# A graph and expert-mixture kernel on one core: in the second graph stage, each panel's products are issued ahead of the rest of the panel before, and the preparation is divided between two engines

## The chip, the cores and the metric

The kernel runs on one core of a Trainium2 chip. The metric is device time in microseconds. Three runs before the change gave 1915.95, 1919.1 and 1920.69 us; the median is 1919.1 us. The engines are PE (matrix products), DVE (vector), ACT (scalar and table functions), POOL (GpSimd) and SP (which here only starts transfers).

## The reference

The input is `x` with 3125 nodes of 256 features, and 50000 edges `src -> dst`. Four blocks follow each other, each of them normalizing `x`, computing something, and adding it to `x`:

```python
x = x + L0_gnn(layernorm(x))     # two mean-aggregating graph convolutions, one product
x = x + L0_ffn(layernorm(x))     # 16 experts, two chosen for each node
x = x + L1_gnn(layernorm(x))     # the second graph stage: the change is here
x = x + L1_ffn(layernorm(x))     # 8 experts, two chosen for each node

# L1_gnn, with P = 64 and K = 3
x_static = x[:, :P]
for i in range(K):               # degree-normalized convolution with self-loops
    x_static = relu(gcn_conv(x_static, src, dst, W_static[i], b_static[i]))
ew = gelu(x @ W1 + b1) @ W2 + b2
x_dyn = segment_sum(x[:, :P][dst] * ew[src], src)
out = concatenate([x_static + x_dyn, x[:, P:]]) @ W_aggr + b_aggr
```

## The kernel before

The nodes are padded to 3200, that is 25 tiles of 128, and grouped in seven panels: six of 512 columns and one of 128. Earlier in the kernel the edges have been counted into a dense matrix of small integers, kept on the chip as 8-bit numbers (`at8`, one tile for each panel). A graph convolution is then a product of the node features with this matrix.

The second graph stage has these parts.

*Preparation* (L1042 to L1052). For each panel the rows are loaded from `xb0` (SP, L1045) and normalized: statistics on DVE (L387, L388), a square root on ACT (L390), a reciprocal (L391) and one subtract-and-multiply for each tile on DVE (L393). POOL's `split` (L428, L429) writes the first 64 features as a rounded number and its remainder into `xc`. Each tile is transposed on PE (L401) and copied by ACT (L402) into `xT`, one tile for all panels. DVE scales the 64 features by `dinv` (L1051), and `split` writes them into `g0`. The rows have two buffers and the scaled features one.

*Branch.* `second_graph` is built twice, for exact and for rounded operands. A flag chooses at run time; the traced execution takes the rounded form. Within the branch ACT first issues the loads of the weights and biases.

*Passes* (three, the loop over `i`). For each panel, PE multiplies 25 blocks of the matrix with the features (`pc`, L1136). Each block of 8-bit numbers is first cast to 32 bits: of five blocks ACT casts two (L434), DVE two (L436) and POOL one (L438); there are five block buffers. The product with the identity (L1142) adds the self-loops. ACT copies `pc` to `gT` (L1147). In passes 1 and 2, four small products with the weights follow (`pw`, L1151), then three steps on DVE (L1156, L1157, L1161: scale, bias, rectify and scale) and POOL's `split` into the features of the next pass. In pass 3 the product is made the other way round, with features along partitions (`pwT`, L1167): `dinv` is spread by four products with the identity (`pi`, L1172), ACT copies it, DVE multiplies, ACT adds the bias and rectifies (L1179), DVE adds the result to `xT` (L1180), and `finish` follows.

*dynamic* runs for four panels after pass 1 and for three after pass 2. It computes `ew` and the dynamic part, for which the matrix is transposed on PE (L474), and writes it over the first 64 features in `xT`.

*finish* makes a panel's output: the rows are loaded again (L1112), `product` with `W_aggr` (`po`, L413), two additions on DVE (L1116 for the bias, L1117), a store, a normalization (into `rows`, one buffer), a store, a transposition of each tile and the gate scores (`pg`, L413; L489), and then the router's `panel` (L526 to L589), a chain of small DVE steps with two small products in it (`ranks`, L568 and L569).

The order on each engine is not that of the source. A scheduler places the instructions of a branch in one fixed order for each engine at build time; at run time each engine takes its own instructions strictly in that order. In pass 3 this order puts `pwT` of a panel directly behind the first `ranks` product of the panel before it.

Of the kernel before, what the change touches and what calls it, by code (L numbers as in the profile page):

```python
# [8 lines left out]
F32 = mybir.dt.float32  # L9
# [9 lines left out]
P = 128  # L19
# [33 lines left out]
def kernel(ctx: ExitStack, tc: tile.TileContext, a, out: bass.AP):  # L53
# [325 lines left out]
            nc.vector.tensor_copy(deg, pdeg)  # L379


    def normalize(dst, x, n):

        mv = work.tile([P, TPP, 2], F32, name="mv")
        st = work.tile([P, TPP, 6], F32, name="st")
        for i in range(n):
            nc.vector.bn_stats(st[:, i, :], x[:, i, :])  # L387
            nc.vector.bn_aggr(mv[:, i, :], st[:, i, :])  # L388
        rstd = work.tile([P, TPP], F32, name="rstd")
        nc.scalar.activation(rstd[:, :n], mv[:, :n, 1], AF.Sqrt, bias=eps)  # L390
        nc.vector.reciprocal(rstd[:, :n], rstd[:, :n])  # L391
        for i in range(n):
            nc.vector.tensor_scalar(  # L393
                dst[:, i, :], x[:, i, :], mv[:, i, 0:1], rstd[:, i : i + 1], op0=OP.subtract, op1=OP.mult
            )

# [10 lines left out]
    def rows_in(ap, c0, w):  # L407
        return ap[c0 : c0 + w, :].rearrange("(t p) d -> p t d", p=P)
# [626 lines left out]

    with ExitStack() as c:
        gp = c.enter_context(tc.tile_pool(name="gp", bufs=1))
        xp = c.enter_context(tc.tile_pool(name="xp1", bufs=2))
        open_rows(c, 1)
        xT = gp.tile([P, KD, NP], F32, name="xT")  # L1040
        g0, g1, xc = (gp.tile([P, NT, 2, CD], F32, name=n) for n in ("g0", "g1", "xc"))
        for c0, w in PANELS:  # L1042
            n, t0 = w // P, c0 // P
            rows = xp.tile([P, TPP, D], F32, name="x")
            nc.sync.dma_start(rows[:, :n, :], rows_in(xb0, c0, w))  # L1045
            normalize(rows, rows, n)
            split(xc[:, t0 : t0 + n, 0, :], xc[:, t0 : t0 + n, 1, :], rows[:, :n, :CD])
            g = xp.tile([P, TPP, CD], F32, name="g", bufs=1)
            for i in range(n):
                transpose_tile(xT[:, :, c0 + i * P : c0 + (i + 1) * P], rows[:, i, :])  # L1050
                nc.vector.tensor_scalar(g[:, i, :], rows[:, i, :CD], dinv[:, t0 + i : t0 + i + 1], None, op0=OP.mult)  # L1051
            split(g0[:, t0 : t0 + n, 0, :], g0[:, t0 : t0 + n, 1, :], g[:, :n, :])  # L1052

        def second_graph(exact):
            one = F32 if exact else F32R
            with ExitStack() as c:
                loads = c.enter_context(tc.tile_pool(name="loads1", bufs=3))
                cw = c.enter_context(tc.tile_pool(name="cw1", bufs=1))
                small = c.enter_context(tc.tile_pool(name="small1", bufs=1))
# [5 lines left out]
                        ws[i * CD : (i + 1) * CD], a["L1_gnn_W_static"].rearrange("i p q -> p i q")  # L1065
                    )
                bs = row_of(cw, "L1_gnn_b_static", 3 * CD)
                bs2 = cw.tile([CD, 1], F32, name="bs2")
                nc.scalar.dma_start(bs2, a["L1_gnn_b_static"][2:3, :].rearrange("i (p o) -> p (i o)", o=1))
                wd1 = weight(cw, "L1_gnn_W1", P)  # L1070
                bd1 = cw.tile([P, 1], F32, name="bd1")
                nc.scalar.dma_start(bd1, a["L1_gnn_b1"].rearrange("(p o) -> p o", o=1))
# [9 lines left out]
                def dynamic(c0, w):  # L1082
# [2 lines left out]
                    pe = ps_one("pe1", [P, PW])  # L1085
                    for k in range(KD):
                        nc.tensor.matmul(  # L1087
                            pe[:, :w], wd1[:, k, :], xT[:, k, c0 : c0 + w], start=(k == 0), stop=(k == KD - 1)
                        )
                    e1 = gw.tile([P, PW], F32, tag="wide", name="e1")  # L1090
                    nc.scalar.activation(e1[:, :w], pe[:, :w], AF.Gelu, bias=bd1)
# [11 lines left out]
                    nc.scalar.copy(both[:, :w], pd[:, :w])  # L1103
                    pf = ps_one("pf", [CD, PW])
                    nc.tensor.matmul(pf[:, :w], fold, both[:, :w], start=True, stop=True)
                    nc.vector.tensor_mul(xT[:CD, 0, c0 : c0 + w], ew[:, :w], pf[:, :w])

                def finish(c0, w):

                    n, t0 = w // P, c0 // P  # L1110
                    x = xp.tile([P, TPP, D], F32, name="x")
                    nc.sync.dma_start(x[:, :n, :], rows_in(xb0, c0, w))  # L1112
                    for i in range(n):
                        po = ps_one("po", [P, D])
                        product(po, xT[:, :, c0 + i * P : c0 + (i + 1) * P], wa)
                        nc.vector.tensor_add(x[:, i, :], x[:, i, :], ba)  # L1116
                        nc.vector.tensor_add(x[:, i, :], x[:, i, :], po)  # L1117
                    nc.sync.dma_start(rows_in(xb1, c0, w), x[:, :n, :])
                    rows = rows_tile()
                    normalize(rows, x, n)  # L1120
                    nc.sync.dma_start(rows_in(xnd1, c0, w), rows[:, :n, :])
                    s = small.tile([P, TPP, NE1], F32, name="s")[:, :n, :]
                    for i in range(n):
                        nT = gw.tile([P, KD, P], F32, name="nT", bufs=1)
                        transpose_tile(nT, rows[:, i, :])
                        scores(s[:, i, :], nT, gw1, gb1, NE1)
                    router1.panel(small, c0, s)

                g = g0
                for i in range(3):  # L1130
                    nxt = g1 if i == 0 else g0
                    for c0, w in PANELS:
                        n, t0 = w // P, c0 // P
                        pc = ps_wide("pc")[:, 0, :]
                        for k, blk in panel_of(exact, loads, c0, w, True):
                            nc.tensor.matmul(  # L1136
                                pc[:, :w], g[:, k].rearrange("p i q -> p (i q)").bitcast(one), blk,
                                start=(k == 0), stop=False,
                            )
                        for t in tiles_of(c0, w):  # L1140
                            o = t * P - c0
                            nc.tensor.matmul(  # L1142
                                pc[:, o : o + P], g[:, t].rearrange("p i q -> p (i q)").bitcast(one), identr.bitcast(one),
                                start=False, stop=(o + P == w),
                            )
                        gT = gw.tile([P, PW], F32, tag="wide", name="gT")
                        nc.scalar.copy(gT[:, :w], pc[:, :w])  # L1147
                        if i < 2:
                            pw = ps_one("pw", [P, TPP, CD])
                            for o in range(n):  # L1150
                                nc.tensor.matmul(  # L1151
                                    pw[:, o, :], gT[:, o * P : (o + 1) * P], ws[:, i, :], start=True, stop=True
                                )
                            s = dinv[:, t0 : t0 + n, None].to_broadcast([P, n, CD])
                            v = gw.tile([P, TPP, CD], F32, name="v")
                            nc.vector.tensor_tensor(v[:, :n, :], pw[:, :n, :], s, OP.mult)  # L1156
                            nc.vector.tensor_tensor(  # L1157
                                v[:, :n, :], v[:, :n, :],
                                bs[:, None, i * CD : (i + 1) * CD].to_broadcast([P, n, CD]), OP.add,
                            )  # L1160
                            nc.vector.scalar_tensor_tensor(  # L1161
                                v[:, :n, :], v[:, :n, :], 0.0, s, op0=OP.max, op1=OP.mult
                            )
                            split(nxt[:, t0 : t0 + n, 0, :], nxt[:, t0 : t0 + n, 1, :], v[:, :n, :])
                        else:
                            pw = ps_one("pwT", [CD, PW])
                            nc.tensor.matmul(pw[:, :w], ws[:, i, :], gT[:, :w], start=True, stop=True)  # L1167

                            pi = ps_one("pi", [CD, PW])
                            for t in tiles_of(c0, w):  # L1170
                                o = t * P - c0
                                nc.tensor.matmul(  # L1172
                                    pi[:, o : o + P], dinv[:, t : t + 1].to_broadcast([P, CD]), ident,
                                    start=True, stop=True,
                                )
                            v = gw.tile([CD, PW], F32, tag="wide", name="vT")
                            nc.scalar.copy(v[:, :w], pi[:, :w])
                            nc.vector.tensor_mul(v[:, :w], v[:, :w], pw[:, :w])
                            nc.scalar.activation(v[:, :w], v[:, :w], AF.Relu, bias=bs2)  # L1179
                            nc.vector.tensor_add(xT[:CD, 0, c0 : c0 + w], xT[:CD, 0, c0 : c0 + w], v[:, :w])  # L1180
                            finish(c0, w)
                    if i < 2:
                        g = nxt
                        for c0, w in PANELS[4 * i : 4 * i + 4]:
# [62 lines left out]
```

## Time and profile before

| | us |
|---|---|
| median of three runs | 1919.1 |
| the profiled execution | 1919.9 |
| its span, first to last instruction | 1918.1 |
| mean granted TensorE clock | 0.92 |
| busy: PE / DVE / ACT / POOL | 1652.2 / 893.1 / 682.5 / 509.8 |
| preparation: first load to last copy | 1079.3 to 1117.5 |
| passes 1, 2, 3: first product | 1130.4, 1279.3, 1394.9 |
| last `po` | 1565.8 |

Times inside a trace are counted from the span's start. A line of the timeline gives start, duration, engine, source line, operation, output and input tile, the count of merged instructions, and in brackets the idle time of the engine before it with the instruction that ended the wait. "x8" on PE means eight passes: a 32-bit product takes two of them.

### The profile page before, as it was taken

The numbers are of one execution on the slowest core, as the hardware profiler recorded it, in microseconds if no ns is written. First come the engines' busy times: TensorE is split into PE (matmuls) and PEld (weight loads), VectorE is DVE, ScalarE is ACT, GpSimd is POOL, SyncE is SP. The second block draws the span as 40 slices with busy tenths as digits, with TensorE's granted clock in tenths as the row PEclk, the third lists the DMA queues.
The fourth block names the chain that finished last, engine by engine and source line by source line (L and its number), as shares of the span: only waits on it lengthen the run. The fifth ranks groups of instructions, "written<-read, shape, count | busy, mean of one in ns | idle before, by whom it ended". The sixth has DMA issues, their size and how long they took to land. (4 is left out here: it accounts for less than half of the span.)

```text
span 1918.1 us, 24044 instructions
## 1 busy us (share of the span) xinstructions
PE 1652.2 (86%) x7618; PEld 1127.4 (59%) x7618; DVE 893.1 (47%) x2509; ACT 682.5 (36%) x1596; POOL 509.8 (27%) x543
## 2 busy tenths in 40 slices
PE   4899999799998399999999459789797647999995
PEld 3777777677777155665556336456565534556553
DVE  5866665246665423322233457456467452222221
ACT  2766666234442122222222246346363102222221
POOL 4411110100000334444443234014021202445442
PEclk9999999999998599999999769999998657999998
DMA  3311111611110687777777220000012603444444
GB/s 116 104 47 47 48 48 37 224 59 56 56 59 24 202 247 216 218 213 211 211 217 192 63 60 0 1 1 1 1 34 66 233 28 76 102 102 99 101 103 102
DMA packets 126765, 193.02 MB, mean 101 GB/s; under 512 B 15040, under 2 KB 71727, under 8 KB 126559
## 3 DMA queue, kind: packets, MB, share of 16 engines
q1 hardware_dynamic: 93036, 137.34, 22.6%
q0 software_dynamic: 28544, 50.74, 12.7%
q10 hardware_dynamic: 5042, 3.23, 0.6%
q8 instruction: 67, 1.10, 0.2%
q14 instruction: 76, 0.61, 0.1%
HBM read 148.74 MB, written 45.72 MB: 101 GB/s over the span
## 5 line engine op out<-in xcount | busy, mean ns | idle before, releaser
L723 PE MATMUL pa<-blk,hl 128*128 128x512 f32 (+1 forms) x1400 | 366.9, 401 | 1.3 <-ACT blk L434 1.3
L997 POOL DMA_INDIRECT xb<-y,idx x120 | 190.9, 1591 | 326.7 <-DVE each L992 221.2
L723 PEld LDWEIGHTS pa<-blk,hl 128*128 128x128 f32 x1400 | 249.3, 196 | 43.7 <-ACT blk L434 1.8
L434 ACT CAST blk<-at 128x512 fp32r<-128x512 fp8e4 (+1 forms) x378 | 208.3, 572 | 137.2 <-PE pa L723 59.4
L961 PE MATMUL ph<-w,xT 128*128 128x512 f32 x512 | 238.8, 610 | 5.6 <-ACT xT L402 0.8
L980 PE MATMUL pe<-w_all,hTs 128*128 x960 | 227.2, 379 | 3.0 <-ACT hTs L976 3.0
L980 PEld LDWEIGHTS pe<-w_all,hTs 128*128 128x128 f32 x960 | 182.1, 190 | 78.1 <-issue 55.5
L436 DVE CAST blk<-at 128x512 fp32r<-128x512 fp8e4 (+1 forms) x392 | 167.8, 438 | 93.2 <-PE pa L723 56.4
L1136 PE MATMUL pc<-blk,g 128*128 128x512 f32 (+1 forms) x525 | 150.2, 420 | 23.9 <-ACT blk L434 13.7
L940 POOL DMA_INDIRECT xg<-xnd,idx x120 | 117.9, 982 | 168.4 <-DVE idx L661 86.0
L961 PEld LDWEIGHTS ph<-w,xT 128*128 128x128 f32 x512 | 92.6, 191 | 114.4 <-issue 88.3
L402 ACT COPY xT<-pt 128x256 f32<-128x256 f32 x195 | 72.6, 372 | 227.8 <-PE pt L401 226.0
L1027 DVE TENSOR_TENSOR hid<-hid,ph 128x512 f32<-128x512 f32 x64 | 44.0, 688 | 232.8 <-ACT hid L1026 232.8
L438 POOL CAST blk<-at 128x512 fp32r<-128x512 fp8e4 (+1 forms) x105 | 66.1, 629 | 292.2 <-PE pc L1136 290.3
L1136 PEld LDWEIGHTS pc<-blk,g 128*128 128x128 f32 x525 | 92.7, 201 | 66.2 <-DVE blk L436 22.3
L1026 ACT ACTIVATE hid<-ph 128x512 f32<-128x512 f32 x64 | 38.2, 597 | 219.4 <-PE ph L961 219.4
L961 PE MATMUL ph<-w_all,xT 128*128 x224 | 112.0, 624 | 4.2
L271 ACT ACTIVATE at<-pcount 128x400 fp8e4<-128x400 f32 x196 | 97.4, 502 | 49.4 <-PE pcount L267 48.2
L267 PE MATMUL pcount<-onehots 128*128 128x100 f16 x784 | 93.8, 270 | 3.0 <-ACT at L271 1.5
L267 PEld LDWEIGHTS <-onehots 128*128 128x128 f16 x784 | 68.8, 118 | 28.3 <-issue 12.8
L906 POOL DMA_DIRECT2D w_all<-in_L_ffn_w_dram x16 | 12.1, 767 | 268.2 <-PE totals L604 263.6
L1209 ACT ACTIVATE hid<-hid 128x512 f32<-128x512 f32 x56 | 35.3, 630 | 133.8 <-DVE hid L1208 133.8
(250 smaller groups left out, 2284.2 us busy)
## 6 DMA issues: line engine op xcount, KB each, us to landing
w<-in_L_ffn_w_dram SPq DMA_DIRECT2D x128, 512.0 KB, 4.7
bin<-in_L_ffn_b_dram SPq DMA_DIRECT2D x56, 256.0 KB, 3.5
w_all<-in_L_ffn_w_dram POOLq DMA_DIRECT2D x16, 512.0 KB, 10.7
w_all<-in_L_ffn_W_dram POOLq DMA_DIRECT2D x16, 512.0 KB, 10.8
h1d<-hl SPq DMA_DIRECT2D x25, 256.0 KB, 2.0
hl<-h1d SPq DMA_DIRECT2D x25, 256.0 KB, 5.3
xp<-in_x_dram SPq DMA_DIRECT2D x12, 512.0 KB, 4.7
mine<-own SPq DMA_DIRECT2D x12, 512.0 KB, 3.9
```

The costliest lines, as they stand in the source:

```text
L267: nc.tensor.matmul(pw[:, w * NF : (w + 1) * NF], ohl[:, b, :, w], ohk[:, b, :, w], start=True, stop=True)
L271: nc.scalar.activation(at8[o // PW][:, :, o % PW : o % PW + 4 * WN].rearrange("p k (w r) -> p w k r", r=WN), pw[:, : 4 * NF].rearrange("p ...
L402: nc.scalar.copy(dst, pt)
L434: nc.scalar.copy(dst, src)
L436: nc.vector.tensor_copy(dst, src)
L438: nc.gpsimd.tensor_copy(dst, src)
L723: nc.tensor.matmul(pa[:, m, :w], parts[k][:, i, m * P : (m + 1) * P].bitcast(one), blk, start=(k == 0 and i == 0), stop=(k == NT - 1 and i ...
L940: nc.gpsimd.indirect_dma_start(out=xg, out_offset=None, in_=xnd[:, :], in_offset=bass.IndirectOffsetOnAxis(ap=idx[:, b : b + 1], axis=0),)
L961: ran.append(nc.tensor.matmul(ph[:, i, :], xT[:, k, :], weight_of(b, weights, i, k), start=(k == 0), stop=(k == KD - 1)))
L980: nc.tensor.matmul(po, hT[:, j, :], weight_of(b, weights, n_in, j), start=(j == 0), stop=(j == n_hid - 1 and b_out is None))
L997: nc.gpsimd.indirect_dma_start(out=xb[:, :], out_offset=bass.IndirectOffsetOnAxis(ap=idx[:, b : b + 1], axis=0), in_=y, in_offset=None, co ...
L1136: nc.tensor.matmul(pc[:, :w], g[:, k].rearrange("p i q -> p (i q)").bitcast(one), blk, start=(k == 0), stop=False,)
```

## The change

1. `normalize` can put every second tile's subtract-and-multiply on POOL; the preparation asks for that.
2. The preparation has four buffers for the rows and for the scaled features. One operation scales a panel's features instead of four. The `split` into `xc` now stands behind the transpositions.
3. `xT` becomes seven tiles, one for each panel. The buffers of the preparation are released before the branch, and `finish` gets two of its own.
4. In every pass the products of a panel (`convolve`) are written ahead of the remaining steps (`weighted`) of the panel before.
5. Pass 3 has the form of the others: `pw`, scale, bias and rectify with rows along partitions, and then a transposition (`pv`) and the addition to `xT`. `pwT`, `pi`, their two ACT steps and the load of `bs2` are gone.

```diff
-    def normalize(dst, x, n):
+    def normalize(dst, x, n, two=False):
...
         for i in range(n):
-            nc.vector.tensor_scalar(
+            (nc.gpsimd if two and i % 2 else nc.vector).tensor_scalar(
                 dst[:, i, :], x[:, i, :], mv[:, i, 0:1], rstd[:, i : i + 1], op0=OP.subtract, op1=OP.mult
             )
...
-        xp = c.enter_context(tc.tile_pool(name="xp1", bufs=2))
         open_rows(c, 1)
-        xT = gp.tile([P, KD, NP], F32, name="xT")
+        xT = [gp.tile([P, KD, w], F32, name=f"xT{c0 // PW}") for c0, w in PANELS]
         g0, g1, xc = (gp.tile([P, NT, 2, CD], F32, name=n) for n in ("g0", "g1", "xc"))
...
+        with ExitStack() as c1:
+            xp = c1.enter_context(tc.tile_pool(name="xp1", bufs=4))
+            for c0, w in PANELS:
+                n, t0 = w // P, c0 // P
+                rows = xp.tile([P, TPP, D], F32, name="x")
+                nc.sync.dma_start(rows[:, :n, :], rows_in(xb0, c0, w))
+                normalize(rows, rows, n, two=True)
+                g = xp.tile([P, TPP, CD], F32, name="g")
+                nc.vector.tensor_tensor(
+                    g[:, :n, :], rows[:, :n, :CD], dinv[:, t0 : t0 + n, None].to_broadcast([P, n, CD]), OP.mult
+                )
+                split(g0[:, t0 : t0 + n, 0, :], g0[:, t0 : t0 + n, 1, :], g[:, :n, :])
+                for i in range(n):
+                    transpose_tile(xT[c0 // PW][:, :, i * P : (i + 1) * P], rows[:, i, :])
+                split(xc[:, t0 : t0 + n, 0, :], xc[:, t0 : t0 + n, 1, :], rows[:, :n, :CD])
...
+                xp = c.enter_context(tc.tile_pool(name="xp1", bufs=2))
...
-                bs2 = cw.tile([CD, 1], F32, name="bs2")
-                nc.scalar.dma_start(bs2, a["L1_gnn_b_static"][2:3, :].rearrange("i (p o) -> p (i o)", o=1))
...
+                def convolve(g, c0, w):
+                    pc = ps_wide("pc")[:, 0, :]
+                    for k, blk in panel_of(exact, loads, c0, w, True):
+                        nc.tensor.matmul(
+                            pc[:, :w], g[:, k].rearrange("p i q -> p (i q)").bitcast(one), blk, start=(k == 0), stop=False
+                        )
...
+                    return pc
+
+                def weighted(i, nxt, c0, w, pc):
...
+                    nc.scalar.copy(gT[:, :w], pc[:, :w])
+                    pw = ps_one("pw", [P, TPP, CD])
+                    for o in range(n):
+                        nc.tensor.matmul(pw[:, o, :], gT[:, o * P : (o + 1) * P], ws[:, i, :], start=True, stop=True)
...
+                    nc.vector.tensor_tensor(v[:, :n, :], pw[:, :n, :], s, OP.mult)
+                    nc.vector.tensor_tensor(
+                        v[:, :n, :], v[:, :n, :], bs[:, None, i * CD : (i + 1) * CD].to_broadcast([P, n, CD]), OP.add
+                    )
+                    if i < 2:
+                        nc.vector.scalar_tensor_tensor(v[:, :n, :], v[:, :n, :], 0.0, s, op0=OP.max, op1=OP.mult)
+                        split(nxt[:, t0 : t0 + n, 0, :], nxt[:, t0 : t0 + n, 1, :], v[:, :n, :])
+                        return
+                    nc.vector.tensor_scalar(v[:, :n, :], v[:, :n, :], 0.0, None, op0=OP.max)
+                    pv = ps_one("pv", [CD, PW])
+                    for o in range(n):
+                        nc.tensor.transpose(pv[:, o * P : (o + 1) * P], v[:, o, :], ident)
+                    x = xT[c0 // PW][:CD, 0, :]
+                    nc.vector.tensor_add(x, x, pv[:, :w])
+                    finish(c0, w)
...
                 for i in range(3):
                     nxt = g1 if i == 0 else g0
+                    before = None
                     for c0, w in PANELS:
...
+                        now = (c0, w, convolve(g, c0, w))
+                        if before:
+                            weighted(i, nxt, *before)
+                        before = now
+                    weighted(i, nxt, *before)
```

More of the change, by code (lines that the diff above doesn't have):

```diff
@@ L1037 @@
         gp = c.enter_context(tc.tile_pool(name="gp", bufs=1))
-        xp = c.enter_context(tc.tile_pool(name="xp1", bufs=2))
         open_rows(c, 1)
-        xT = gp.tile([P, KD, NP], F32, name="xT")
+        xT = [gp.tile([P, KD, w], F32, name=f"xT{c0 // PW}") for c0, w in PANELS]
         g0, g1, xc = (gp.tile([P, NT, 2, CD], F32, name=n) for n in ("g0", "g1", "xc"))
[L1042 to L1052, printed above, removed]
+        with ExitStack() as c1:
[13 more added lines that the diff above has]
+                split(xc[:, t0 : t0 + n, 0, :], xc[:, t0 : t0 + n, 1, :], rows[:, :n, :CD])
         def second_graph(exact):
@@ L1087, in dynamic @@
                         nc.tensor.matmul(
-                            pe[:, :w], wd1[:, k, :], xT[:, k, c0 : c0 + w], start=(k == 0), stop=(k == KD - 1)
+                            pe[:, :w], wd1[:, k, :], xT[c0 // PW][:, k, :], start=(k == 0), stop=(k == KD - 1)
                         )
@@ L1105, in dynamic @@
                     nc.tensor.matmul(pf[:, :w], fold, both[:, :w], start=True, stop=True)
-                    nc.vector.tensor_mul(xT[:CD, 0, c0 : c0 + w], ew[:, :w], pf[:, :w])
+                    nc.vector.tensor_mul(xT[c0 // PW][:CD, 0, :], ew[:, :w], pf[:, :w])
                 def finish(c0, w):
@@ L1114, in finish @@
                         po = ps_one("po", [P, D])
-                        product(po, xT[:, :, c0 + i * P : c0 + (i + 1) * P], wa)
+                        product(po, xT[c0 // PW][:, :, i * P : (i + 1) * P], wa)
                         nc.vector.tensor_add(x[:, i, :], x[:, i, :], ba)
@@ L1127, in finish @@
                     router1.panel(small, c0, s)
+                def convolve(g, c0, w):
[4 more added lines that the diff above has]
+                        )
+                    for t in tiles_of(c0, w):
+                        o = t * P - c0
+                        nc.tensor.matmul(
+                            pc[:, o : o + P], g[:, t].rearrange("p i q -> p (i q)").bitcast(one), identr.bitcast(one),
+                            start=False, stop=(o + P == w),
+                        )
+                    return pc
+                def weighted(i, nxt, c0, w, pc):
+                    n, t0 = w // P, c0 // P
+                    gT = gw.tile([P, PW], F32, tag="wide", name="gT")
+                    nc.scalar.copy(gT[:, :w], pc[:, :w])
+                    pw = ps_one("pw", [P, TPP, CD])
+                    for o in range(n):
+                        nc.tensor.matmul(pw[:, o, :], gT[:, o * P : (o + 1) * P], ws[:, i, :], start=True, stop=True)
+                    s = dinv[:, t0 : t0 + n, None].to_broadcast([P, n, CD])
+                    v = gw.tile([P, TPP, CD], F32, name="v")
+                    nc.vector.tensor_tensor(v[:, :n, :], pw[:, :n, :], s, OP.mult)
+                    nc.vector.tensor_tensor(
+                        v[:, :n, :], v[:, :n, :], bs[:, None, i * CD : (i + 1) * CD].to_broadcast([P, n, CD]), OP.add
+                    )
+                    if i < 2:
[9 more added lines that the diff above has]
+                    finish(c0, w)
                 g = g0
@@ L1131, in second_graph @@
                     nxt = g1 if i == 0 else g0
+                    before = None
                     for c0, w in PANELS:
[L1133 to L1181, printed above, removed]
```

## The prediction

> **What bounds the kernel now.** I cut the span into stages first, because the change touches only the second graph stage (1079 to 1576 us; the columns are engine busy times, granted TensorE clock, DMA share).
>
> ```profile
> 1079.00:1118.00 39.00, 12.56 (x50) 9.07 (x50) 28.92 (x107) 11.38 (x32) 15.08 (x29) 0.50 0.29 98
> 1118.00:1130.40 12.40, 0.00 (x0) 0.02 (x1) 0.43 (x2) 0.75 (x2) 0.12 (x1) 0.50 0.40 108
> 1130.40:1191.00 60.60, 56.48 (x248) 39.87 (x249) 44.33 (x97) 40.57 (x77) 29.31 (x46) 0.92 0.01 1
> 1395.00:1455.00 60.00, 54.41 (x252) 38.33 (x250) 45.21 (x142) 37.16 (x69) 17.00 (x25) 0.97 0.17 53
> 1455.00:1500.00 45.00, 34.37 (x145) 24.80 (x145) 29.53 (x114) 13.12 (x32) 4.92 (x11) 0.77 0.16 52
> 1500.00:1576.00 76.00, 42.54 (x139) 29.36 (x138) 38.10 (x164) 8.88 (x22) 11.10 (x15) 0.55 0.45 154
> ```
>
> Four different limits. The panel preparation (1079 to 1118) runs at DVE's pace. Then PE stands for 12.4 us: engines come through the branch and ACT issues its weight loads before its first cast. Passes 1 and 2 (1130 to 1191 is pass 1) are PE-bound. Pass 3 (1395 to 1576) is a chain of tails: no engine is full after 1455 and the clock falls to 0.55.
>
> In pass 1 the timeline shows one small hole per panel:
>
> ```profile
> 1152.19 2.56 PE L1136 MATMUL pc<-blk,g 128*128 128x512 f32 x9
> 1155.11 3.62 PE L1136 MATMUL pc<-blk,g 128*128 128x512 f32 x12 [0.36 <-DVE blk L436]
> ...
> 1154.22 3.33 DVE L436 CAST blk<-at 128x512 fp32r<-128x512 fp8e4 x5
> ...
> 1153.97 0.80 POOL L438 CAST blk<-at 128x512 fp32r<-128x512 fp8e4 x1 [0.62 <-PE pc L1136]
> 1154.72 0.58 POOL L428 CAST g<-v 128x256 fp32r<-128x256 f32 x1
> 1155.39 0.80 POOL L429 TENSOR_TENSOR g<-v,g 128x256 fp32r<-128x256 f32 x1
> ```
>
> PE takes a block in 2.56/9 = 0.285 us and waits 0.36 us where DVE's casts take 3.33/5 = 0.67 us instead of the 0.43 us they take elsewhere: POOL is busy beside them. A panel lasts 8.55 us, so 8.19 without the hole.
>
> In pass 3, one tail with no products left to hide it:
>
> ```profile
> 1508.23 0.21 PE L568 MATMUL ranks<-both,tri 128*128 128x32 f16 x1 [3.96 <-DVE both L564]
> 1508.37 1.97 PE L1167 MATMUL pwT<-gT,ws 128*64 128x512 f32 x2
> 1510.41 1.97 PE L1172 MATMUL pi<-ident,dinv 128*64 128x128 f32 x8
> 1515.23 6.71 PE L413 MATMUL po<-w_L_gnn_W_aggr,xT 128*128 128x256 f32 x16 [2.85 <-DVE xT L1180]
> 1535.83 0.21 PE L568 MATMUL ranks<-both,tri 128*128 128x32 f16 x1 [3.54 <-DVE both L564]
> ```
>
> Each tail's `pwT` stands on PE behind the `ranks` of the tail before, which waits for that tail's last router step on DVE. So pass 3 is the first product (9 us), then six links of 25 to 28 us and a short last one. The products fit beside the first links; what counts is where the first tail begins and how long a link is.
>
> **Preparation.** Half of L393 goes to POOL, the four `g` scalings of a panel become one, four buffers let panels 3 and 4 load without waiting.
>
> ```profile
> 1089.09 2.15 DVE L393 TENSOR_SCALAR x<-x,mv,rstd 128x256 f32<-128x256 f32 x4
> 1111.96 1.38 DVE L393 TENSOR_SCALAR x<-x,mv,rstd 128x256 f32<-128x256 f32 x4
> 1113.26 1.44 DVE L1051 TENSOR_SCALAR g<-x,dinv 128x64 f32<-128x64 f32 x4
> 1121.87 2.13 ACTq L1064 DMA_DIRECT2D ws<-in_L_gnn_W_static_dram  x2
> ```
>
> A panel now takes 5.05 us (the L393 groups start at 1101.87, 1106.91, 1111.96), plus 3 to 4 us at 1091 to 1097 waiting for panel 3's load. After: DVE 1.74 (statistics) + 0.18 + 0.70 (two L393) + 0.42 (one 128x256 TENSOR_TENSOR, as L1116) = 3.0 us. POOL: its splits, 0.41 + 0.74 + 0.40 + 0.72 = 2.27 us, plus two L393. The trace has no POOL TENSOR_SCALAR. Bounds: POOL's one-input CAST of this shape, 0.41 us, and its two-input TENSOR_TENSOR, 0.73 us. I take 0.5, near the cast, since it has one tensor input (the Trainium skill, GPSIMD Engine Reference, section 4.1, calls one-input operations roughly line rate). So POOL 3.3 us.
>
> The rule that speaks against this is in the Trainium skill, SBUF — State Buffer, section Who interferes with whom: DVE and GpSimd share a port pair under an exclusive lock, taken by DVE for two-port TENSOR_SCALARs and for operations with two SBUF inputs. By the rule POOL's 3.3 us and DVE's 1.1 us add: 4.4 us a panel. The first row above agrees on DVE's side (2.15 against 1.38, with POOL active), but POOL's own 0.72 us stayed 0.72. I take 3.9. First statistics end near 1087 as now; POOL's first four L393 end at 1089.4, two panels' splits at 1094.0, panel 3's L393 at 1095.0, then 3 x 3.9: 1106.7; transposes and copies add 1.8: 1108.5 against 1117.5 now, -9.0. (With 3.3: -10.8; with 4.4: -7.5; with POOL at 0.73: -5.) POOL order and branch delay (ACT 1117.5 to 1121.9) stay. ACT issues one load fewer, `bs2`, 0.7 us of its 7.8. **Preparation: -9.7 us** (-13 to -5). SP gains nothing else: the first loads for `finish` stand behind the release of the preparation's buffers (near 1108) and land before DVE's L1118, which waits for `ba` anyway.
>
> **Passes 1 and 2.** A panel's products come ahead of `pw` of the panel before. DVE's three steps on `v` are now spaced by casts and start 0.23 us after the next panel's first block. I count from that block. `v` ends near 2.5 us. In the new POOL order the split stands after two casts instead of three: 2.5 + 0.67 + 0.74 = 3.9, and POOL's cast of block 14 (0.80 beside DVE) ends at 4.7. PE wants block 14 at 14 x 0.285 = 4.0. DVE's contended casts of 11 and 13 cost no more than 0.1 before. So the hole of 0.36 closes and one of about 0.75 opens, whose releaser is POOL: +0.4 in each of panels 3 to 6, -0.36 in panel 2 (no split beside it), +0.4 in the narrow panel 7 (0.9 of holes now, 1.3 then). 4 x 0.4 - 0.36 + 0.4 = 1.6 a pass: **+3.3 us** for two. Ends: no hole, 12 x -0.36 = -4; the whole split visible (1.4), +12. Between the passes `dynamic` follows two `v` chains (2.1 us on DVE) that lie beside the 2.5 us of `pe1`: nothing.
>
> **Pass 3.** The new PE order puts all of panel 2's products, then `pw`, nine blocks of panel 3, `pv`, four blocks, before the first `po`. Product 1 ends 9.1 us after the pass starts; 25 x 0.285 + 0.39 + 0.85 = 8.4; 2.6; `pv`, eight 128-column matmuls like `pi`, 1.0; 1.1: `po` at 22.3 us. Now it is 1410.3 - 1394.9 = 15.4. **+6.9**, in full on the chain. A link from there:
> - ranks to next `po` (now 6.6, 8.4, 7.7, 7.0, 7.0). The new form: `pw` (eight loads of 128 columns, 1.0; 2.0 at the low clock as `pg` shows, 1.02 for four), DVE 0.42 + 0.29 + 0.42 + 0.22 + 0.25, `pv` 1.0 to 2.0, L1168 0.68. Bare: 6.6 against 7.0; where the scaling waited behind `onehots` (L589, 1.29 us) and casts: -1.0, -1.7, -1.0. ACT's two steps and `pi` go, but three DVE steps and `pv` stand in their place. Sum: -4.5.
> - `po` to ranks: in links 1 and 2 two DVE casts more (+0.9, +0.65). Products end one panel earlier in the chain, so tail 3 runs like tail 4 now (17.3 for 15.4) and tail 4 bare (18.4 for 17.0); the reason is PE's clock: `po` takes 3.61 us at 1410 and 6.71 at 1515. Sum +4.9, with the last tail +0.4: +5.3.
>
> Together 6.9 - 4.5 + 5.3: **+7.5 us** (0 to +12). Seven tiles for xT: same bytes, and no wait on xT in the trace but on its true producer; nothing.
>
> **Sum.** -9.7 + 3.3 + 7.5 = +1.1 us on the profiled execution (span 1918.1, 1919.9 with what lies around it), which is 0.8 above the median of 1919.1. So 1920.2 us for the median; I say 1920. A measurement of this kernel can tell about 0.3%, 5.8 us, from nothing.
>
> **Rivals.**
> - *POOL and DVE hardly disturb each other* in the new orders. For it: POOL's SUB kept 0.72. Preparation at 3.3 us a panel (-11.5), no hole in passes 1 and 2 (-4), pass 3 +7.5: -8, 1911. Against it: casts at 0.67 beside a split.
> - *The late first tail is repaid*: DVE casts less in the links (products are through earlier), the six links shrink by 1.2 us each, pass 3 ends at +0.5: -6, 1913. Against it: links 4 to 6 have no casts now and are the longest.
> - *Slower: POOL's split before the third cast.* Place: block 14 of panels 3 to 7, both passes. If `v` ends 0.5 us later than I have it (DVE's `v` steps took 0.75 where POOL was active), the hole is 1.2 to 1.4: +11 for +3.3, sum +9, 1928. It decides from a hole of 1.2 us a panel on.
> - *No effect on the links*: the DVE chain alone sets them, -4.5 falls away: 1924.5, inside the bound of no change.
>
> **Chances.** No measurable change 0.42 (my sum and the last rival); the two faster rivals and a better preparation 0.33 (I leave room there, since an order made for overlap may hide more than I see); slower 0.25. The likeliest case's own range is 1914 to 1926. For 8 in 10 I reach to a fast end with preparation at -13 and no holes (1906, less a little) and to the slow rival: 1905 to 1930.
>
> **What would show it.** Preparation: last `xT` copy near 1108, POOL TENSOR_SCALAR near 0.5 us; PE's first `pc` near 1121. Passes: the hole in `pc` names POOL's L438 or nothing. Pass 3: first `po` 22 us after the pass begins; `ranks` to `ranks` of 25 to 28 us; clock at 0.55 over more than 76 us. I am wrong if POOL's L393 costs 1 us or more, if the hole in passes 1 and 2 is above 1.2 us or absent, or if the links fall below 25 us.

## The result, and the profile after

The changed kernel took 1913.2 us (median of 8 runs, 1907.5 to 1914.2), the kernel before 1919.0 us beside it: ratio 0.9965, 95% interval 0.995 to 0.9979. A second comparison gave 1910.1 us (22 runs) against 1915.7 us: ratio 0.9976, interval 0.9966 to 0.9986. So the change makes the kernel 5 to 6 us faster, about the 0.3% that can be told from nothing. The forecast was 1920, no change.

The stages of the changed kernel, in the columns of the first table of before (busy times of PE, PE's weight loads, DVE, ACT, POOL; granted clock, DMA share, GB/s). The stages are the preparation, PE's standstill at the branch, pass 1, and pass 3 in three parts:

```profile
1077.00:1115.00 38.00, 15.08 (x50) 8.19 (x50) 21.05 (x77) 10.76 (x32) 28.93 (x37) 0.50 0.37 116
1115.00:1125.00 10.00, 0.00 (x0) 0.00 (x0) 0.43 (x2) 0.58 (x2) 1.64 (x5) 0.50 0.34 75
1125.00:1186.80 61.80, 56.13 (x250) 40.05 (x251) 41.57 (x95) 43.22 (x80) 28.56 (x45) 0.91 0.01 2
1391.60:1450.00 58.40, 55.45 (x265) 40.76 (x265) 44.34 (x138) 38.28 (x71) 18.48 (x27) 0.97 0.16 49
1450.00:1500.00 50.00, 34.69 (x145) 27.19 (x143) 30.61 (x127) 9.12 (x25) 14.77 (x23) 0.67 0.61 211
1500.00:1570.00 70.00, 37.55 (x136) 27.75 (x136) 38.19 (x171) 4.92 (x15) 0.00 (x0) 0.57 0.16 55
```

The first row is the surprise. Before, DVE was busy for 28.9 of 39 us and POOL for 15.1. Now POOL is busy for 28.9 of 38 us and DVE for 21.1: the bound moved from one engine to the other, and the stage is hardly shorter.

Where the time went, from two profiled executions of each kernel (first / second, in us):

| stage | before | after | mean change | forecast |
|---|---|---|---|---|
| first load to last `xT` copy | 38.2 / 38.1 | 37.8 / 37.8 | -0.4 | -9.0 |
| last `xT` copy to PE's first `pc` | 12.95 / 11.6 | 10.4 / 10.4 | -1.9 | -0.7 |
| pass 1, first `pc` to first `pe1` | 61.7 / 61.2 | 61.7 / 61.9 | +0.4 | +1.6 |
| first `dynamic` (four panels) | 87.2 / 88.2 | 88.65 / 88.7 | +0.9 | 0 |
| pass 2 | 58.8 / 58.8 | 59.0 / 59.1 | +0.2 | +1.6 |
| second `dynamic` (three panels) | 56.8 / 57.0 | 57.1 / 57.1 | +0.2 | 0 |
| pass 3, first `pc` to the router's first `nodes` product | 189.8 / 187.85 | 186.7 / 183.2 | -3.9 | +7.5 |
| sum (of unrounded figures) | | | -4.3 | +1.1 |

The sum is near the measured 5 to 6 us. The two executions of one kernel differ by up to 3.5 us in a stage, so a difference of 1 or 2 us between single traces means nothing by itself.

By stage the forecast is furthest off in pass 3 (three terms, 11.4 us); the largest error of a single term is the preparation's, 8.6 us. The same line on both engines (least, median and most ns), and how long DVE's `g` waited for POOL (us in all, waits):

```profile
L393 DVE TENSOR_SCALAR x<-x,mv,rstd x13: 401/498/885, 1085.2 to 1113.0; 128x256 f32<-128x256 f32 x13
L393 POOL TENSOR_SCALAR x<-x,mv,rstd x12: 1212/1222/1476, 1085.1 to 1111.4; 128x256 f32<-128x256 f32 x12
  DVE g L1049: 11.4, 6
```

POOL needs 1.22 us where I took 0.5 with an upper bound of 0.73. DVE does the same work in 0.4 to 0.5. Two panels in the timeline of the changed kernel:

```profile
1094.70 2.42 POOL L393 TENSOR_SCALAR x<-x,mv,rstd 128x256 f32<-128x256 f32 x2
1097.16 0.43 DVE L1049 TENSOR_TENSOR g<-x,dinv 128x256 f32<-128x256 f32 x1 [2.62 <-POOL x L393]
1099.78 2.46 POOL L393 TENSOR_SCALAR x<-x,mv,rstd 128x256 f32<-128x256 f32 x2
1102.28 0.42 DVE L1049 TENSOR_TENSOR g<-x,dinv 128x256 f32<-128x256 f32 x1 [2.00 <-POOL x L393]
```

The first of these pairs takes POOL 2.42 us although DVE stands idle all that time (2.62 us), so this is POOL's own speed and not a contest with DVE for a port. POOL's period is 5.1 us a panel, as long as DVE's was before (5.05).

In pass 1 the hole is where the forecast put it, and behind POOL's cast of block 14:

```profile
1152.61 4.03 PE L1134 MATMUL pc<-blk,g 128*128 128x512 f32 x14
1157.48 2.97 PE L1134 MATMUL pc<-blk,g 128*128 128x512 f32 x11 [0.84 <-POOL blk L438]
...
1155.27 0.53 POOL L428 CAST g<-v 128x256 fp32r<-128x256 f32 x1 [0.34 <-DVE v L1160]
1155.88 0.80 POOL L429 TENSOR_TENSOR g<-v,g 128x256 fp32r<-128x256 f32 x1
1156.62 0.81 POOL L438 CAST blk<-at 128x512 fp32r<-128x512 fp8e4 x1
```

POOL has the two steps of the split in hand until 1156.6; the cast that PE needs starts then, and PE waits 0.84 us (0.75 was forecast, in place of 0.36).

And one link of pass 3 with no products beside it, to be read beside the link of before; the last line is `pv` in the first tail, where PE's clock is up:

```profile
1506.53 0.21 PE L568 MATMUL ranks<-both,tri 128*128 128x32 f16 x1 [3.34 <-DVE both L564]
1506.57 1.95 PE L1152 MATMUL pw<-ws,gT 128*128 128x64 f32 x8
1510.47 1.03 PE L1166 MATMUL pv<-ident,v 128*64 128x128 f32 x4 [1.17 <-DVE ranki L577]
1512.27 5.10 PE L413 MATMUL po<-w_L_gnn_W_aggr,xT 128*128 128x256 f32 x16 [0.77 <-DVE xT L1168]
...
1410.56 0.63 PE L1166 MATMUL pv<-ident,v 128*64 128x128 f32 x4
```

From `ranks` to `po` it takes 5.7 us; before it took 7.0. `pv` has four passes, one for each tile: a transposition of 32-bit numbers takes one pass here, where a product takes two (`pw`, x8).

### The profile page after: what moved, and what is told of

It reads as the page before. It is cut to its first block, busy times and chain, and to the rows that moved or that the text cites. A ratio compares the mean times of both kernels' runs of the same rounds, so it can differ in the third digit from the quotient of the medians.

```text
span 1911.3 us, 24068 instructions
## 1 busy us (share of the span) xinstructions
PE 1651.0 (86%) x7629; PEld 1128.0 (59%) x7629; DVE 879.7 (46%) x2493; ACT 676.6 (35%) x1582; POOL 524.2 (27%) x555
## 5 line engine op out<-in xcount | busy, mean ns | idle before, releaser
L1134 PE MATMUL pc<-blk,g 128*128 128x512 f32 (+1 forms) x525 | 145.5, 416 | 23.7 <-ACT blk L434 11.4
L1026 ACT ACTIVATE hid<-ph 128x512 f32<-128x512 f32 x64 | 38.2, 597 | 218.9 <-PE ph L961 218.9
```

The costliest lines, as they stand in the source:

```text
L1134: nc.tensor.matmul(pc[:, :w], g[:, k].rearrange("p i q -> p (i q)").bitcast(one), blk, start=(k == 0), stop=False)
```

## The experiments

All were timed beside the kernel before. The changed kernel is at 0.9965 and 0.9976 of it, about 1912 us on the scale of these comparisons. The two theories that I started from: *A*, POOL's L393 spoils the preparation, and pass 3 gained by its new form in spite of the new order; *B*, something else bounds the preparation, and the new order shortened the links of pass 3.

**L393 on DVE alone.**

```diff
-                normalize(rows, rows, n, two=True)
+                normalize(rows, rows, n)
```

> The changed kernel with one part undone: in the preparation DVE does all of L393 again, POOL none. Theory A (POOL's L393 takes 1.25 us each and POOL's 5.1 us a panel set the pace): a panel falls to DVE's statistics 1.74 + 0.18 + four L393 1.38 + scaling 0.42 = 3.7 us, so four panels at 1.4 us less and the first pair without 5.17 us on POOL; the last xT copy comes 30 to 33 us after the first load issue, where the changed kernel has it at 37.8, and the time is 5 to 8 us below the changed kernel, 1905 to 1908. Theory B (the pace is set by DVE, by the loads or by the transpositions, and POOL's share is relief): the last copy stays at 37 to 41 us, and the time is 0 to 3 us above the changed kernel, 1913 to 1916.

Measured: 1902.4 us, ratio 0.992 (0.9904 to 0.9936). The last `xT` copy comes 29.8 us after the first load, 8.0 us earlier than in the changed kernel, and PE's first `pc` 8.6 us earlier. DVE's L393 in this kernel:

```profile
1095.22 1.65 DVE L393 TENSOR_SCALAR x<-x,mv,rstd 128x256 f32<-128x256 f32 x4
1099.25 1.37 DVE L393 TENSOR_SCALAR x<-x,mv,rstd 128x256 f32<-128x256 f32 x4
1102.64 1.56 DVE L393 TENSOR_SCALAR x<-x,mv,rstd 128x256 f32<-128x256 f32 x4
```

The period is 3.4 to 4.0 us a panel. Theory A holds. What else is new in the preparation (buffers, merged scaling, the later `split`; not separated here) is worth some 8 us, and the half on POOL took all of it away again.

**The old preparation in the changed kernel.** Two buffers, four scalings, the old sequence and all L393 on DVE (parts 1 and 2 of the change, reversed); the preparation's buffers are still released ahead of the branch.

> The changed kernel with the old preparation: two buffers for the rows, one for the scaled features, four scalings a panel, all L393 on DVE, xc split ahead of the transpositions. xT in seven tiles, order and form stay. If the preparation brought what the traces show from the first load to the first product (51.2 to 48.2 us), this is 3 us above the changed kernel, 1916; if part of the 3 us belongs to the branch (ACT's wait of 4.4 became 2.55 us) and not to the order of the preparation, it is 1 us above it; if my prediction's 9.7 us were right after all and hidden by something later, it is near 10 us above it.

Measured: 1912.7 us, ratio 0.9978 (0.9967 to 0.9989), the same as the changed kernel within the intervals. Last `xT` copy at 38.2 us, gap to `pc` 10.5 us. The new preparation as it was made is worth nothing that can be measured, and the shorter gap does not come from it.

**The old order in all passes, and in pass 3 alone.**

```diff
-                        now = (c0, w, convolve(g, c0, w))
-                        if before:
-                            weighted(i, nxt, *before)
-                        before = now
-                    weighted(i, nxt, *before)
+                        weighted(i, nxt, c0, w, convolve(g, c0, w))
```

> The changed kernel with the old order in all three passes: each panel's remaining steps stand directly behind its own products; preparation and the new form of pass 3 stay. Theory A (the new form of pass 3, not the order, shortened the links): the first po comes 15 to 16 us after pass 3 starts instead of 20.4, the stretch from ranks to the next po stays at 5 to 6 us, passes 1 and 2 lose the POOL hole and get the DVE hole back (0 to -2 us); sum 2 to 7 us below the changed kernel, 1906 to 1911. Theory B (the order shortened the links, because all products are out of the way earlier): ranks to po goes back to 6.5 to 8.5 us in the first three links, and the time is 0 to 5 us above the changed kernel, 1913 to 1918.

For pass 3 alone, the loop calls `weighted` at once if `i == 2`.

> The changed kernel with the old order in pass 3 alone; passes 1 and 2 keep the new one. Passes 1 and 2 must read as in the changed kernel (61.7 and 59.0 us from first product to the first pe1). Theory A: pass 3 gets 3 to 5 us shorter from its first product to the first nodes product (186.7 in the changed kernel), 1908 to 1910. Theory B: pass 3 gets 0 to 5 us longer, 1913 to 1918. The distance to the kernel with the old order throughout is the worth of the order in passes 1 and 2: by the traces 0 to 1 us.

Measured: 1907.0 us (0.994, 0.9926 to 0.9954) and 1906.9 us (0.9937, 0.9924 to 0.995). Pass 3 lasts 181.0 and 181.7 us with the first `po` at 14.3 and 14.7 us, and the stretches from `ranks` to `po` remain short, 31.1 and 29.8 us in sum against 30.1 in the changed kernel and 39.4 before. The form shortened them, not the order; theory B falls. Passes 1 and 2 together take 120.2 us in the old order and 121.0 in the new: the order is worth nothing there, in this kernel.

**The old form of pass 3 in the new order.** `weighted` makes `pwT`, `pi` and ACT's two steps if `i == 2`, as before; the `bs2` load returns.

> The changed kernel with pass 3 in its old form (pwT, pi, ACT's two steps, the bs2 load) but in the new order; all else stays. Theory A (the form shortens each link by taking serial steps out of it, whatever the order): the stretches from ranks to the next po go back to 6.5 to 8.5 us, pass 3 lasts 194 to 197 us from its first product to the first nodes product (186.7 in the changed kernel), and the time is 8 to 10 us above the changed kernel, 0.3% above the kernel before. Theory B (the form is worth only the 4.5 us of my sum): pass 3 lasts 190 to 192 us, the time is 4 to 5 us above the changed kernel and the same as before.

Measured: 1923.7 us, ratio 1.0029 (1.002 to 1.0038). Pass 3 lasts 198.7 us, longer than expected. A bare link:

```profile
1513.48 0.21 PE L568 MATMUL ranks<-both,tri 128*128 128x32 f16 x1 [3.96 <-DVE both L564]
1513.62 1.97 PE L1154 MATMUL pwT<-gT,ws 128*64 128x512 f32 x2
1515.66 1.97 PE L1158 MATMUL pi<-ident,dinv 128*64 128x128 f32 x8
1520.73 6.01 PE L413 MATMUL po<-w_L_gnn_W_aggr,xT 128*128 128x256 f32 x16 [3.10 <-DVE xT L1166]
```

7.25 us against 5.74, with the order unchanged. The first two stretches, where products compete, are 10.2 and 9.2 us against 4.8 and 5.7. So for pass 3 as a whole (us, means of the profiled executions that have the combination):

| | old order | new order |
|---|---|---|
| old form | 188.5 (three) | 198.7 (one) |
| new form | 181.6 (five) | 185.5 (five) |

The order costs 4 us with the new form and 10 with the old. The form gains 7 us with the old order and 13 with the new.

**The rounding half of the split on ACT, in passes 1 and 2.**

```diff
-                        split(nxt[:, t0 : t0 + n, 0, :], nxt[:, t0 : t0 + n, 1, :], v[:, :n, :])
+                        nc.scalar.copy(nxt[:, t0 : t0 + n, 0, :].bitcast(F32R), v[:, :n, :])
+                        nc.gpsimd.tensor_sub(
+                            nxt[:, t0 : t0 + n, 1, :].bitcast(F32R), v[:, :n, :], nxt[:, t0 : t0 + n, 0, :]
+                        )
```

> The changed kernel with one step moved in passes 1 and 2: the rounding half of the split (a cast of 128x256) goes from POOL to ACT; POOL keeps the subtraction. Theory A (the hole of 0.84 us in panels 3 to 6 is POOL's cast of block 14 held up by the split): it shrinks by POOL's cast of 0.53 us to 0.3 us or less, a panel takes 8.4 to 8.5 us instead of 8.93, and the two passes together are 4 to 6 us shorter. Theory B (ACT has no room, 6.5 of 8.9 us are taken): ACT's casts come late instead, the hole names ACT, and the passes gain 0 to 2 us. The rest reads as in the changed kernel.

Measured: 1898.7 us, ratio 0.9898 (0.9883 to 0.9912). The hole is gone altogether. Panels 2 and 4 of pass 1 in the changed kernel, engine by engine (columns as in the first table):

```profile
1136.27:1143.24 6.97, 6.97 (x36) 5.22 (x35) 4.39 (x10) 6.29 (x11) 3.12 (x6) 1.00 0.01 2
1151.75:1160.69 8.94, 8.10 (x40) 5.51 (x39) 6.50 (x13) 6.38 (x11) 4.77 (x8) 1.00 0.00 0
```

and panel 4 with the rounding on ACT:

```profile
1148.48:1156.28 7.80, 7.80 (x40) 5.56 (x39) 5.71 (x13) 6.70 (x12) 4.42 (x7) 1.00 0.00 0
```

ACT took one instruction more and had the room. The panel is 1.14 us shorter: 0.84 is the hole, 0.30 is PE's own busy time (8.10 to 7.80), and DVE's fell by 0.8 us. Passes 1 and 2 take 58.0 and 53.4 us, 9.4 to 9.7 less than in the changed kernel, twice what I expected. The time fell by 13 to 15 us; of the rest, pass 3 (183.2 us here, in code that is the same) shows that much scatter, and I can't say more of it.

**The same in the old order.**

> The old order in all three passes and the rounding half of the split on ACT; all else as in the changed kernel. The question is what the new order is worth in passes 1 and 2 once the split no longer holds up POOL's cast. Theory A (the order lets PE run at its own pace, 0.24 us a block, and the hole hid this): with the old order a panel still takes 8.3 to 8.5 us, pass 1 lasts 60 to 61 us and pass 2 57 to 58 us (58.0 and 53.4 with the new order), and the time is 2 to 4 us below the kernel with the old order and the split on POOL. Theory B (the order is worth nothing, only POOL's load counts): a panel takes 7.8 us here too, pass 1 about 58 us and pass 2 about 53.5 us.

Measured: 1902.2 us, ratio 0.9923 (0.9902 to 0.9944), 3 us below the old order with the split on POOL (the intervals overlap). Passes 1 and 2: 60.3 and 57.65 us, a panel 8.34 us, still with DVE's hole of 0.36. So both passes together, in us:

| | split on POOL | rounding on ACT |
|---|---|---|
| old order | 120.2 | 118.0 |
| new order | 121.0 | 111.3 |

With the rounding on ACT the order is worth 6.6 us; with the whole split on POOL it is worth nothing. Each figure is of one or two traces, but a full panel repeats within 0.02 us in each: 8.55 and 8.34 us in the old order, 8.94 and 7.80 in the new one (panels 4 to 6).

**Tiles and release alone, in the kernel before.** `xT` in seven tiles, the preparation's buffers released ahead of the branch, nothing else.

> The kernel before with nothing but xT in seven tiles and the preparation's buffers released ahead of the branch. Theory A (this shortened the gap from the last xT copy to PE's first product, 12.95 us before and 10.4 in the changed kernel): the gap falls to 10 to 11 us here, and the time is 2 us below the kernel before. Theory B (the gap's change comes from the missing bs2 load, 0.67 us, and from where the instructions of the branch come to lie): the gap stays at 12 to 13 us or takes some other value, and the time is within 1.5 us of the kernel before. In both, passes and tails read as before.

Measured: 1917.4 us, ratio 0.9994 (0.9986 to 1.0002). No effect on the time, as forecast for the tiles, though the gap in this one trace was 10.9 us.

**Both kernels once more.**

> The kernel before, unchanged, for a second profiled execution. In the first, the gap from the last xT copy to PE's first product was 12.95 us and the first load of the stage started at 1079.25 us; in the changed kernel 10.4 us and 1076.9. Theory A (these two differences come from the one execution that was profiled, since the kernel with tiles only had a gap of 10.9 us and no gain in time): the second profile shows other values, the gap anywhere from 10 to 13 us, the load start from 1074 to 1080. Theory B (the gap is a property of the program): 12.5 to 13.4 us again. Pass 3 and its links must repeat, 187 to 190 us, with one link or another 2 us shorter where PE's clock happens to be up.

> The changed kernel, unchanged, again, beside the kernel before on the same chip. If the execution profiled first is typical: load to last xT copy 37.8 us, gap 10 to 11 us, pass 1 61.5 to 62, pass 3 183 to 187 us (the kernel with the rounding on ACT had 183.2 for the same pass 3), and the time 0.3 to 0.5% below the kernel before.

Measured: 1917.4 us for the kernel before, one run, and 1910.1 us for the changed one (the ratio is above). The first load of the stage starts between 1074.4 and 1079.8 us in the fourteen profiled executions, in code that is the same: of the 2.4 us by which it was earlier in the first trace after, nothing need be the change's. The gap: 12.95, 11.6, 11.3 and 10.9 us in the four executions that load `bs2`, 9.8 to 11.1 us (mean 10.4) in the nine without it that issue their loads in the branch. The means differ by 1.3 us, of which 0.7 is the load's own issue; why the rest, and why it scatters so with the load in place, stays open. In pass 3 it is the links that scatter: link 5 took 20.6 us from `po` to `ranks` in the first trace before and 18.35 in the second.

**Put together.** All L393 on DVE, the old order in pass 3 alone, the rounding on ACT.

> A version put together from what the first runs showed: the changed kernel with all L393 on DVE, the old order in pass 3 alone, and the rounding half of the split on ACT in passes 1 and 2. If the parts add: 8.5 us (L393 on DVE) plus 5 us (order of pass 3) plus 4 to 6 us (split) below the changed kernel, 1891 to 1896. If the earlier preparation is partly given back (pass 1 was 1.4 us longer with L393 on DVE), or the split gains nothing, 1897 to 1900.

Measured: 1893.4 us, ratio 0.9866 (0.9852 to 0.9881). The three parts, each alone below the changed kernel, come to 27 us or more; 19 to 21 are left. By the trace the parts are there: first `pc` 7.3 us earlier, passes 9.5 us shorter, pass 3 2.7 us below the mean of its form and order (182.8 for 185.5), 19.5 us in sum, which is what is measured. It is the single comparisons that show more than their stages (13 to 15 us for 9.4 with the rounding on ACT); I put that down to scatter, which is argued and not shown.

**The weight loads ahead of the preparation.** In the combined version the gap is 11.1 us, of which ACT spends 6.7 us on issuing loads. Its source has them in the branch; here they stand in front of the preparation's loop, in the same words.

> The combined version with the loads of the second graph stage's weights and biases issued by ACT ahead of the preparation instead of inside the branch. Theory A (between the last xT copy and PE's first product ACT's issues take 7 to 9.5 us of the 9 to 12 us): the gap falls to 2 to 5 us, and the time is 6 to 8 us below the combined version, 1885 to 1888. Theory B (the gap belongs to the branch[...]): the gap stays at 7 us or more, and the time is within 3 us of the combined version. If the early issues hold up ACT's first square root instead, the last xT copy moves from 29.8 to 32 us and takes 2 us of the gain back.

Measured: 1883.0 us, ratio 0.9824 (0.9802 to 0.9845), 34 us below the kernel before. PE's first product in it, and what DVE waited for in the combined version (last line):

```profile
1114.21 4.21 PE L1133 MATMUL pc<-blk,g 128*128 128x512 f32 x9 [4.69 <-ACT blk L434]
...
1121.81 1.43 DVE L1118 TENSOR_TENSOR x<-x,row_L_gnn_b_aggr 128x256 f32<-128x256 f32 x4 [8.36 <-DMA row_L_gnn_b_aggr<-in_L_gnn_b_aggr_dram]
```

PE's wait of 11.5 us has become 4.7, most of which lies at the branch, where DVE and ACT start nothing for 4.0 and 3.6 us; what fills that time the trace does not show. The early issues do hold up ACT's first square root (last `xT` copy at 32.0 instead of 29.9 us), which takes back 2 us. The time fell by 10 us, more than the 6 to 8 expected. PE's first `pc` comes 4.7 us earlier after the first load, and pass 1 is 3.3 us shorter (54.5 for 57.9), 1.9 of it in the first panel: in the combined version DVE's casts stand there behind an addition of `finish` (L1118) that waits for the load of `b_aggr`, and that load now lands early. This version beats both kernels.

## Why the prediction was wrong

It forecast no change, from -9.7, +3.3 and +7.5. Measured are -2.2, +0.6 and -3.9, and +1.1 in `dynamic`. No term had the right size, and the errors of the first and the last had opposite signs: that 1913 came within 7 us of 1920 is luck.

*Preparation.* The step that failed is "I take 0.5, near the cast, since it has one tensor input", and its bounds with it: 1.22 us lies outside both. The nearest rows in the trace were of other operations, and I let the number of inputs decide which row was near. The Trainium skill's sentence (GPSIMD Engine Reference, section 4.1, one-input operations "roughly line-rate") fits the cast's 0.40 us and not this operation, a subtract-and-multiply with two scalars for each row. The measurement decides. The text itself named the point: "I am wrong if POOL's L393 costs 1 us or more." With L393 on DVE the last copy comes 8.4 us earlier than before. That this is near the -9.0 of the forecast does not confirm the sum: the forecast had half of L393 on POOL, and this kernel comes to about the same 3.4 to 4.0 us a panel without it. The exclusive lock that I weighed (SBUF — State Buffer, Who interferes with whom) is not what bounds the stage. POOL's L393 has its 1.22 us with DVE idle beside it. Some contention shows on DVE, whose L393 has a mean of 0.57 us here and 0.46 without POOL's share.

*Branch.* I kept the delay and took 0.7 us for `bs2`; the gap shrank by 1.9 us, by 1.3 over all executions.

*Passes 1 and 2.* Place, cause and size of the new hole were right (0.84 for 0.75, in panels 3 to 6). Two terms were mis-sized. In panel 2 I had only the hole of 0.36 go; the panel fell by 1.6 us (6.97 for 8.55). About 0.4 of this is no gain, since half of panel 1's `pw` now stands behind panel 2; over the pass one whole `pw` moves to the end, which is 1.0 us longer. The rest, some 0.8 us, is the pace. I had taken 2.56/9 = 0.285 us a block for PE's own pace (the second group in the same lines gives 3.62/12 = 0.30). Panel 2 has no steps on `v` and no `split` beside its casts, and there the same division gives 4.68/18 = 0.26:

```profile
1138.33 4.68 PE L1134 MATMUL pc<-blk,g 128*128 128x512 f32 x18
```

So the 0.285 was in part the casts' pace. PE's own line had no gap for it, but its weight loads in panel 4 of the kernel before name a cast:

```profile
1156.52 0.19 PEld L1136 LDWEIGHTS pc<-blk,g 128*128 128x128 f32 x1 [0.42 <-DVE blk L436]
```

The second term is the narrow panel 7: +0.4 forecast, some -0.4 and -0.3 measured in the two passes. With these two terms the passes come to the +0.4 and +0.2 of the table, for +1.6 each.

*Pass 3.* The late first tail was right in kind: +4.8 for +6.9. Panel 2's products with `pw` took 7.4 us instead of 8.4, and `pv` 0.4 instead of 1.0. The step that failed in the links is the price of `pv`: "eight 128-column matmuls like `pi`", 1.0 us or 2.0 at the low clock. It has four passes, not eight, and takes 0.6 and 1.03 us. A bare stretch from `ranks` to `po` was therefore 5.75 to 5.86 us and not 6.6, and the sum of the stretches from `ranks` to `po` was -9.4 (39.5 to 30.1) where I had -4.5. `pv` accounts for up to 1 us of this in each of five links; what is left was not divided further. The second half of the sum, +5.3 from `po` to `ranks`, was +0.7. Link 3 did get longer (means 16.5 to 19.2, +1.9 forecast), but link 4 kept its 19.2 (+1.4 forecast), and links 5 and 6 lost 1 us each, where I had nothing. That 1 us is within what one link scatters between two executions of the same kernel (2.2 us); why link 4 did not grow stays open. From `ranks` to `ranks`, three links of the first trace fell below the 25 us that I had named as a sign of being wrong (22.7, 24.9 and 24.1; the first link of before was 24.8).

*Rivals.* "POOL and DVE hardly disturb each other", 1911, needed 3.3 us a panel and no hole; it was 5.1, and the hole is there. "The late first tail is repaid", 1913, gave the time but not the mechanism: it looked to fewer casts in the links, and the form did it, in the old order as well. "No effect on the links" is refuted. The slow rival needed a hole of 1.2 us and got 0.84.

## What to carry to other kernels

Don't move half of an operation to another engine before you know its price there for this very operation: a row of the same shape but of another operation is no bound. Where two engines share a step and a third waits for both, the slower half sets the pace. When a reordering brings nothing, look at the one wait that names another engine: here a small step on POOL stood in front of a cast, and moving it released what the order was worth. And count the passes of a new product from the nearest operation of its own kind: `pv` is a transposition, and the transpositions in the trace of before (`pt`) had one pass each. A pace read from a busy engine is that engine's own only if what feeds it has time to spare.

## What the runs showed of the hardware

POOL's subtract-and-multiply with two scalars for each row takes 1.22 us on 128x256 32-bit numbers, three times its cast of as many numbers (0.40 for `g`) and more than its two-input subtraction (0.73); DVE needs 0.40 to 0.5. What makes it so dear on POOL was not tested. The pace of a chain of products can be in part that of the casts that feed it while PE counts as busy (0.285 against 0.26 us a block at the same granted clock of 1.00). A transposition of four 32-bit tiles took four passes on PE (`pv`, 1.03 us at the low clock) where a product over four tiles took eight (`pi`, 1.97). In the thinly used tails of pass 3 PE's clock isn't settled: link 5 took 18.4 us from `po` to `ranks` in the kernel with the old order in pass 3 alone, with a granted clock of 0.83 in its first 10 us, and 20.6 us in the first trace before, with 0.67 and 0.50 in its two halves; which link is the short one differs from execution to execution.
